# A graph layer on one core: keys by VectorE's own division, constants and first moments in waits for edges, 24 rows compacted aside behind pass 4

## The chip, the core and the metric

The kernel runs on one core of a Trainium2 chip. A core has engines that run side by side, each through its own list of instructions in order: TensorE (PE in the profile, its weight loads PEld), VectorE (DVE), ScalarE (ACT), GpSimd (POOL) and SyncE (SP). SyncE only issues DMA transfers here. GpSimd issues those whose addresses come from a table (indirect gathers) and those that add to what is there. An engine waits for another by semaphores.

The metric is the time of one execution on the device in microseconds (us). Smaller is better.

## What is computed

`N` is 6250 nodes with 128 channels, `E` 206250 edges sorted by `dst`. Cut to what matters:

```python
def _L0_gnn_ref(x, W, b, edge_index):
    src, dst = (edge_index[0], edge_index[1])
    x_i = x[dst]
    x_j = x[src]
    feat = jnp.concatenate([x_i, x_j - x_i], axis=-1)
    msg = feat @ W.T + b
    out = jax.ops.segment_max(msg, dst, num_segments=x.shape[0])
    return jnp.where(jnp.isfinite(out), out, 0.0)
h = jnp.maximum(_layernorm(x, axis=-1), 0.0)
x = x + _L0_gnn_ref(h, L0_gnn_W, L0_gnn_b, edge_index)
```

The message of an edge is A(dst) + B(src), with A = h (W1 - W2)^T + b and B = h W2^T. So the largest message of a node is its A plus the channelwise maximum of B over its sources.

## The kernel before

Partition p owns 49 consecutive destination nodes. Their edges lie together, since edges are sorted by destination, and partition p loads a window of 1792 edges that covers them. Most edges are handled without any gather: sources are numbered as l times 50 plus q (l up to 125, q up to 50), and for each q TensorE builds, by one-hot matrices, the row of B that each destination wants from that q, and VectorE takes maxima. That works for one edge for each destination and q. The edges left over (a second edge of the same destination and q) are rows that GpSimd gathers from B in DRAM, up to 420 for each partition, and VectorE chains them.

The program order is written out by hand: each engine gets its instructions in the order in which the code issues them. The parts are these.

**Edges.** A coarse look at `dst` gives each partition's window start `begin_i` (lines 271 to 278). GpSimd gathers the windows `swin` (src) and `dwin` (dst), lines 284 and 285. SyncE writes one word of each back (line 340), which holds the later loads of x behind the windows.

**Keys.** For each edge, VectorE and ScalarE make l, q and the destination's place `dlc` among the 49, and from them the key `KA` = 64 dlc + q2 (lines 483 to 498). ScalarE computes `big`, the quotient that VectorE rounds to `vm` (line 490). `T` in the trace is the store `T3`, whose parts (`eq`) hold the integer temporaries, and later the comparison results.

**Comparisons.** 41 lags: VectorE compares `KA` with itself shifted by the lag (line 535), TensorE adds the results up in PSUM `dup` by a matmul with the identity (line 524). At hand-chosen lags (`among`, from line 560) other work is laid between: the moments for the next 10 columns of x (`moments`: bn_stats, bn_aggr), the root and reciprocal (`scales`, `inverse`), and, by `ln(n)`, the next `n` steps of the layer norm and the product.

**Layer norm and product.** `micro` is a list of 75 steps, three to a cycle: `turn` (transposes of two columns), `product` (a bias matmul and two with `wT`, giving B in the first 128 columns and A in the last), `remainder`. Six of the steps run before the comparisons, 40 in them, the others behind. Every ten columns SyncE writes B to `Bt` and A to `XA`, and GpSimd adds x to `XA` (`add_x`).

**Compaction.** ScalarE counts the left-over edges (line 594). A scan gives each the distance it has to move, and eleven passes (`pass_`, lines 632 and 633) move them by 1, 2, 4 and so on. Ahead of pass 6 (`EP` = 6, `early`) the first `EW` = 48 rows (`GB` = 6 groups of `U` = 8) are taken aside out of blocks of 128 and put together in a tree of copies. Their list goes to `ridx` (line 655), and GpSimd issues their gathers while the passes go on. The full list follows at line 717. `turned` transposes the keys on TensorE through a PSUM pool of two tiles (`ps_t`).

**Checks.** Counts in `badc` tell whether the inputs fit the fast path (`finite`, `found`, `apart`, lines 731 to 765).

**Main loop.** 325 pairs (13 tiles of nodes, 25 pairs of q). For each pair: one-hots by TensorE and ScalarE (lines 905, 906), products (line 983), maximum on VectorE (989). `more_rows(to)` lays between them `stream_step`, VectorE's chain over gathered rows (line 157), up to row `to`, and further gathers. Gathered rows live in a ring of `GB` groups in `X`: the next group is issued when the oldest group has been chained, and SyncE copies a chained group to `M` (line 164). `pieces` makes the one-hot inputs OHQ and OHD on VectorE (lines 800 to 807). At last 49 gathers bring the results `R` out of `M` (`get_rows`), VectorE joins them with the main loop's maxima and x (lines 1021, 1022), and SyncE and ScalarE store them.

Of the kernel before, what the change touches and what calls it, by code (L numbers as in the profile page):

```python
# [8 lines left out]
F32 = mybir.dt.float32  # L9
# [10 lines left out]
P = 128  # L20
# [18 lines left out]
U = 8  # L39
# [14 lines left out]
def gnn_kernel(tc, x, src, dst, W, b, out):  # L54
# [17 lines left out]
    EP = 6  # L72
    EW = GB * U
    SETS = (WIN - EW - (1 << EP)) // (2 << EP) + 1
    assert EW + (1 << EP) <= 2 << EP and SETS <= 16 and WIN % (2 << EP) == 0
# [17 lines left out]
    with ExitStack() as ctx:  # L93
# [13 lines left out]
        with ExitStack() as body:  # L107
# [58 lines left out]
            with ExitStack() as pre:  # L166
# [77 lines left out]
                kbias = pool.tile([P, 1], F32, name="kbias")  # L244
                bsel = pool.tile([P, L], F32R, name="bsel")
                brow = pool.tile([P, 2 * C], F32R, name="brow")
                V.memset(kbias, (1 - Q) * 0.5 / Q)
# [37 lines left out]
                gather(dwin, dst.rearrange("(e o) -> e o", o=1), begin_i[:, 0:1])  # L285

# [35 lines left out]
                moments(0, GQ)  # L322
                scales(0, GQ)()
                V.tensor_copy(identb, ident)
                neg = pool.tile([P, P], BF16, name="neg")
                V.tensor_scalar_mul(neg, identb, -100.0)
                negb = pool.tile([P, P], BF16, name="negb")
                V.tensor_scalar_mul(negb, identb, -1.0)
# [3 lines left out]
                V.tensor_copy(IQ, row[:, 0, :Q].rearrange("p (q o) -> p q o", o=1).to_broadcast([P, Q, NBLK]))  # L332
                V.tensor_copy(IL, row[:, 1, :LD].rearrange("p (q o) -> p q o", o=1).to_broadcast([P, LD, NBLK]))
                for i in range(NBLK):
                    V.tensor_scalar_add(IW[:, :, i], row[:, 1, :WN], float(near[i]))
                V.tensor_scalar(nbias, row[:, 0], -2.0, -1.0, op0=ALU.mult, op1=ALU.add)
# [94 lines left out]
                def product(k):  # L431
                    pm = steps[k]["pm"] = ps_m.tile([P, 2, 2 * C], F32, name="pm")
                    T_.matmul(pm[:L], bsel, brow.rearrange("k (o c) -> k o c", o=1).to_broadcast([P, 2, 2 * C]),
                              start=True, stop=False)
                    for j in range(2):
                        T_.matmul(pm[:L, j], hT[k % 2][:, j, :L], wT, start=False, stop=j == 1)  # L436
                    if k + 1 < NP_:
                        scaled(k + 1)
                    g, o = where(k)
                    A_.copy(Bp[:L, 0, 2 * k:2 * k + 2], pm[:L, :, :C])  # L440
                    A_.copy(stage[:, g, o:o + 2], pm[:L, :, :C])
# [31 lines left out]
                scaled(0)  # L473
                ln(2)

# [7 lines left out]
                A_.activation(big, sq, AF.Identity, scale=1.0 / Q, bias=kbias)  # L483
                A_.activation(s16, sq, AF.Identity, bias=nthr)
                V.tensor_scalar(d16, dwin, nthr, None, op0=ALU.add)
                V.tensor_scalar(dlc, d16, 0.0, float(LD + 1), op0=ALU.max, op1=ALU.min)
                dlc64 = eq[0].bitcast(I16)
                lq = eq[1].bitcast(I16)
                V.tensor_scalar(dlc64, dlc, 64.0, None, op0=ALU.mult)
                V.tensor_scalar(vm, big, MAGIC, -(MAGIC + L), op0=ALU.add, op1=ALU.add)  # L490
                V.tensor_scalar(lq, vm, float(-Q), None, op0=ALU.mult)
                V.tensor_tensor(q2, s16, lq, ALU.add)
                V.tensor_tensor(KA[:, 64:], dlc64, q2, ALU.add)
                ln(2)
                A_.activation(big, sq, AF.Copy, scale=float(1 << PB))
                ln(2)
# [68 lines left out]
                among[4] += [sel_rows]  # L565
                later = {}
                for q0, at_ in ((GQ, (1, 2, 3, 5)), (2 * GQ, (8, 10, 11, 13)), (3 * GQ, (17, 19, 20, 22)),
# [5 lines left out]
                for i in range(1, 41):  # L573
                    among[i].append(lambda: ln(1))
# [16 lines left out]
                less = junk[0]  # L591
                for i in range(2):
# [3 lines left out]
                make_sel(30, 40)  # L596

# [39 lines left out]
                def early():  # L637
# [3 lines left out]
                    F, FM = (swin[:, j * 16 * EW:(j + 1) * 16 * EW].rearrange("p (m w) -> p m w", w=EW) for j in range(2))  # L641
# [15 lines left out]
                    for _ in range(GB):  # L657
                        gather_group()
# [22 lines left out]
                for i in range(5):  # L681
                    rest[i].append(lambda i=i: ln(4 if i < 4 else len(micro)))
# [13 lines left out]
                for i in range(11):  # L696
# [3 lines left out]
                    for f in rest[i]:  # L700
# [17 lines left out]
                                op1=ALU.bitwise_and)  # L718
                sdl = u[:, OV:GR + OV]
# [5 lines left out]
                V.tensor_scalar(s, s, -0.5, FMAX, op0=ALU.add, op1=ALU.mult)  # L725
                make_sel(40, Q)
# [4 lines left out]
                spread_begin()  # L731
                finite(w_sb, 2 * C, P, 18)
                finite(bsrc[:1], C, 1, 20)
                found()
                apart()
# [3 lines left out]
                V.tensor_scalar(badc[:, 4:5], over_, 0.0, None, op0=ALU.is_lt)  # L739
                V.tensor_tensor(less[:, 1:], d16[:, 1:], d16[:, :WIN - 1], ALU.is_lt)  # L740
# [11 lines left out]
                for v, op, o in ((VMAX, ALU.is_lt, badc[:L, 16:17]), (-VMAX, ALU.is_gt, badc[:L, 17:18])):  # L752
                    V.tensor_scalar(fin_[:L, :Q], mv[:, :, 1], v, None, op0=op, op1=ALU.add, accum_out=o)
# [346 lines left out]
```

## Time and profile before

| what | us |
|---|---|
| median of three runs (771.83 to 774.6) | 774.47 |
| the profiled execution's own time | 775.43 |
| its span, from the first instruction to the last | 773.6 |
| busy: TensorE / VectorE / ScalarE / GpSimd | 642.1 / 720.9 / 482.9 / 504.0 |
| edges' windows asked for (GpSimd) | 10.99 and 12.41 |
| first comparison (VectorE) | 29.91 |
| first pass | 101.81 |
| first row gather (GpSimd) | 128.79 |
| first maximum of the main loop (VectorE) | 176.82 |
| last row gather, last result gather (GpSimd) | 722.97, 763.78 |

A row of a timeline reads: start and duration in us, engine, line of the code, operation, output and input with their shapes, the count, and in brackets the idle time of the engine just before it with what ended it ("issue" where the profile shows nothing that it waited for). A row that merges several neighbours gives the time of all of them. A row of a group gives the count, the busy time in all, the mean of one in ns, and behind the bar the idle time before them. The engine with the highest busy share need not be the one that sets the end. That is told by who waits for whom, and where.

### The profile page before, as it was taken

How to read it: one execution, taken by the hardware profiler on the slowest of the kernel's cores; microseconds unless marked ns; L12 is line 12 of the kernel's file. 1: busy time of each engine (PE TensorE's matmuls, PEld its weight loads, DVE VectorE, ACT ScalarE, POOL GpSimd, SP SyncE). 2: the span in 40 equal slices, each digit the busy share in tenths (PEclk: the TensorE clock that was granted, in tenths of full speed). 3: DMA queues.
4: the chain of work that ended last, by engine and by line, in shares of the span. 5: the costliest groups of instructions: out<-in, count | busy, mean ns of one | idle time of the engine just before them, and what ended most of it. 6: DMA issues, size and time to landing. Idle time of an engine off the chain costs nothing.

```text
span 773.6 us, 11963 instructions
## 1 busy us (share of the span) xinstructions
PE 642.1 (83%) x3643; PEld 466.6 (60%) x3643; DVE 720.9 (93%) x1304; ACT 482.9 (62%) x1035; POOL 504.0 (65%) x522
## 2 busy tenths in 40 slices
PE   0799884649999898899989898999989898996860
PEld 0455553537667676666767666766767576775750
DVE  6999799987999999999999999999999999997773
ACT  3655683226789999565666657575666667674500
POOL 4000003877777777777777777777777777777764
PEclk9999997759999999999999999999999999998875
DMA  6542444123443433334343243434343233433593
GB/s 196 133 101 67 101 104 108 46 61 94 109 116 103 117 104 92 104 106 116 106 117 101 83 114 104 116 106 115 104 116 101 83 113 103 116 106 106 160 227 123
DMA packets 83699, 85.05 MB, mean 110 GB/s; under 512 B 9996, under 2 KB 71554, under 8 KB 83372
## 3 DMA queue, kind: packets, MB, share of 16 engines
q1 hardware_dynamic: 66951, 47.36, 21.7%
q0 software_dynamic: 16080, 35.93, 17.5%
q10 hardware_dynamic: 596, 0.92, 0.4%
q8 instruction: 30, 0.49, 0.3%
q14 instruction: 42, 0.34, 0.1%
HBM read 46.76 MB, written 40.47 MB: 113 GB/s over the span
## 4 chain that ended last, share of the span: by engine, by line
DVE 25%; PE 16%; issue 15%; ACT 9%; DMA 9%; POOL 3%; DVEq 0%; POOLq 0%
DVE acc L989 15%; PE ps L983 9%; DVE X L157 6%; DMA X<-Bt,ridx 6%; ACT oh L906 5%; PE z L905 4%; ACT counted L996 4%; DMA R<-M,last_e 3%; PE pv L837 2%; POOL X L87 2%; POOL R L87 1%; DVE OHQ L800 1%; DVE acc L987 1%; DVE OHD L807 1%; DVE OHD L804 0%
## 5 line engine op out<-in xcount | busy, mean ns | idle before, releaser
L87 POOL DMA_INDIRECT X<-Bt,ridx x420 | 440.7, 1049 | 131.7 <-issue 45.4
L906 ACT ACTIVATE oh<-z 126x490 fp32r<-126x490 f32 (+1 forms) x650 | 340.1, 586 | 162.6 <-PE z L905 161.3
L983 PE MATMUL ps<-oh,Bp 126*128 126x490 f32 (+1 forms) x1300 | 392.5, 425 | 40.1 <-DVE acc L989 38.9
L989 DVE TENSOR_TENSOR acc<-acc,ps 128x980 f32<-128x980 f32 (+1 forms) x312 | 361.1, 1157 | 8.3 <-PE ps L983 6.8
L983 PEld LDWEIGHTS ps<-oh,Bp 126*128 126x128 f32 x1300 | 239.3, 193 | 135.0 <-DVE acc L989 90.8
L905 PE MATMUL z<-Vb,Sel 128*126 128x490 f16 (+1 forms) x650 | 195.3, 375 | 12.4 <-ACT oh L906 9.7
L157 DVE SCALAR_TENSOR_TENSOR X<-X,slim 128x128 f32<-128x128 f32 x419 | 146.8, 350 | 9.2 <-issue 7.6
L905 PEld LDWEIGHTS <-Sel 128*126 128x126 f16 x650 | 86.8, 142 | 32.1 <-issue 3.9
L837 PEld LDWEIGHTS <-OHQ 128*128 128x128 bf16 x910 | 62.5, 161 | 17.8 <-issue 16.9
L837 PE MATMUL pv<-OHD,OHQ 128*128 128x28 bf16 (+1 forms) x896 | 67.2, 228 | 4.5 <-DVE OHD L807 4.4
L444 POOL DMA_DIRECT2D XA<-in_x x5 | 4.5, 902 | 94.3 <-DMA XA<-acc 94.3
L800 DVE TENSOR_TENSOR OHQ<-T,IQ 128x1092 bf16<-128x1092 bf16 (+5 forms) x104 | 62.2, 605 | 0.0
L87 POOL DMA_INDIRECT R<-M,last_e x49 | 48.3, 985 | 17.0 <-issue 11.3
L996 ACT ACTIVATE counted<-lane_dl,nbias 128x556 bf16<-128x556 int32 x50 | 42.6, 851 | 0.1
L524 PE MATMUL dup<-T,identb 128*128 128x512 bf16 (+1 forms) x168 | 39.8, 363 | 3.0 <-DVE T L535 2.8
L436 PE MATMUL pm<-wT,hT 128*125 128x256 f32 x100 | 27.7, 402 | 2.7 <-ACT hT L425 2.6
L524 PEld LDWEIGHTS <-identb 128*128 128x128 bf16 x168 | 16.2, 99 | 18.8 <-issue 6.4
L633 DVE COPY_PREDICATED pk<-big,pk 128x1927 int32<-128x1927 int32 (+12 forms) x13 | 22.9, 1759 | 0.4
L436 PEld LDWEIGHTS pm<-wT,hT 128*125 128x125 f32 x100 | 19.5, 198 | 6.1 <-ACT hT L425 3.7
L419 ACT ACTIVATE hs<-X,nmr,rstd 125x128 f32<-125x128 f32 x50 | 22.0, 494 | 0.5 <-DVE nmr L306 0.5
L535 DVE TENSOR_TENSOR T<-KA,KB 128x1792 bf16<-128x1792 int16 x21 | 21.5, 1081 | 0.2 <-PE dup L524 0.2
L535 DVE TENSOR_TENSOR T<-KA 128x1792 bf16<-128x1792 int16 x20 | 20.8, 1080 | 0.0
(272 smaller groups left out, 452.1 us busy)
## 6 DMA issues: line engine op xcount, KB each, us to landing
M<-X SPq DMA_DIRECT2D x52, 512.0 KB
X<-Bt,ridx POOLq DMA_INDIRECT x420, 2.5
XA<-in_x POOLq DMA_DIRECT2D x5, 625.0 KB, 6.1
ownb<-Bt SPq DMA_DIRECT2D x12, 245.0 KB
X<-in_x SPq DMA_DIRECT2D x5, 560.0 KB
Bt<-acc SPq DMA_DIRECT2D x4, 560.0 KB
XA<-acc SPq DMA_DIRECT2D x4, 560.0 KB
out_x<-R SPq DMA_DIRECT2D x8, 224.0 KB
```

Source lines behind the costliest of these rows:

```text
L87: G_.indirect_dma_start(out=o, out_offset=None, in_=table, in_offset=bass.IndirectOffsetOnAxis(ap=idx, axis=0))
L157: V.scalar_tensor_tensor(G[:, j], state["prev"], slim[:, k:k + 1], G[:, j], op0=ALU.min, op1=ALU.max)
L436: T_.matmul(pm[:L, j], hT[k % 2][:, j, :L], wT, start=False, stop=j == 1)
L524: T_.matmul(dup[:, c0:c1], w, e[:, c0:c1], start=first, stop=last)
L535: V.tensor_tensor(e, KA[:, 64:], i1, ALU.is_equal)
L800: V.tensor_tensor(OHQ[:, :nl, a:z], over(TQ, z - a), iq, ALU.is_equal)
L837: T_.matmul(o, w, m, start=False, stop=True, skip_group_check=True)
L905: T_.matmul(z[:L + 1, :n], Sel[:, i + j], Vb[t % 2][:, :n], start=True, stop=True)
L906: A_.activation(oh[:, :n], z[:L + 1, :n], AF.Relu)
L983: T_.matmul(ps[:, j, :n], Bp[:, e, i + j], oh[j][:, :n], start=e == 0, stop=e == 1)
L989: V.tensor_tensor(a, a, ps[:, :, :n], ALU.max)
L996: A_.activation(counted.bitcast(BF16)[:, :NS], lane_dl, AF.Sign, scale=2.0, bias=nbias[:, c:c + 1], accum_out=ends[:, c:c + 1])
```

## The change

It changes eight things.

1. The quotient is no longer ScalarE's: VectorE divides `swin` and writes int16, which rounds (`l16`); `lq`, `q2` and `vm` come from it. `KA` is built in place. ScalarE's first pass in this part is now `s16`. The pass that writes `big` for the packed word moves to lag 7.
2. The constants (identb, neg, negb, IQ, IL, IW, nbias) go from behind the first moments to right behind the edges' gathers.
3. The first ten moments are split: five before the keys, five among them, and the scales behind.
4. No layer-norm step runs before the comparisons; inside, each of the 41 lags has one step and every fifth two (49 instead of 40).
5. `EP` 5, `EW` 24: the first 24 rows are taken aside behind pass 4, out of blocks of 64. The other three groups of the ring are issued behind the full list.
6. The checks of W, of the variances and the matmul of `spread_begin` move to the wait for the count; the check of the heads moves ahead, the others change their order.
7. The bias matmul covers only the columns of A.
8. `more_rows` takes 4 rows instead of 10 before the first pair, and then reaches 16 by the fourth pair.

```diff
-    EP = 6
-    EW = GB * U
+    EP = 5
+    EW = 3 * U
...
                 gather(dwin, dst.rearrange("(e o) -> e o", o=1), begin_i[:, 0:1])
+                V.tensor_copy(identb, ident)
...
+                V.tensor_copy(IQ, row[:, 0, :Q].rearrange("p (q o) -> p q o", o=1).to_broadcast([P, Q, NBLK]))
...
-                moments(0, GQ)
-                scales(0, GQ)()
-                V.tensor_copy(identb, ident)
...
+                moments(0, GQ // 2)
...
-                    T_.matmul(pm[:L], bsel, brow.rearrange("k (o c) -> k o c", o=1).to_broadcast([P, 2, 2 * C]),
-                              start=True, stop=False)
+                    T_.matmul(pm[:L, :, C:], bsel, brow[:, C:].rearrange("k (o c) -> k o c", o=1).to_broadcast([P, 2, C]),
+                              start=True, stop=False, skip_group_check=True)
...
-                scaled(0)
-                ln(2)
...
-                A_.activation(big, sq, AF.Identity, scale=1.0 / Q, bias=kbias)
+                lq = eq[1].bitcast(I16)
+                l16 = eq[0].bitcast(I16)
                 A_.activation(s16, sq, AF.Identity, bias=nthr)
+                V.tensor_scalar(l16, sq, 1.0 / Q, (1 - Q) * 0.5 / Q, op0=ALU.mult, op1=ALU.add)
+                V.tensor_scalar(lq, l16, float(-Q), float(Q * L), op0=ALU.mult, op1=ALU.add)
+                V.tensor_tensor(q2, s16, lq, ALU.add)
+                V.tensor_scalar(vm, l16, float(-L), None, op0=ALU.add)
+                moments(GQ // 2, GQ)
+                scaling = scales(0, GQ)
                 V.tensor_scalar(d16, dwin, nthr, None, op0=ALU.add)
                 V.tensor_scalar(dlc, d16, 0.0, float(LD + 1), op0=ALU.max, op1=ALU.min)
-                V.tensor_scalar(dlc64, dlc, 64.0, None, op0=ALU.mult)
-                V.tensor_scalar(vm, big, MAGIC, -(MAGIC + L), op0=ALU.add, op1=ALU.add)
-                V.tensor_scalar(lq, vm, float(-Q), None, op0=ALU.mult)
-                V.tensor_tensor(q2, s16, lq, ALU.add)
-                V.tensor_tensor(KA[:, 64:], dlc64, q2, ALU.add)
-                ln(2)
-                A_.activation(big, sq, AF.Copy, scale=float(1 << PB))
-                ln(2)
+                scaling()
+                scaled(0)
+                V.tensor_scalar(KA[:, 64:], dlc, 64.0, None, op0=ALU.mult)
+                V.tensor_tensor(KA[:, 64:], KA[:, 64:], q2, ALU.add)
...
+                among[7] += [lambda: A_.activation(big, sq, AF.Copy, scale=float(1 << PB))]
...
-                for i in range(1, 41):
-                    among[i].append(lambda: ln(1))
+                for i in range(SH):
+                    among[i].append(lambda i=i: ln(2 if i % 5 == 4 else 1))
...
+                spread_begin()
...
                 make_sel(30, 40)
+                finite(w_sb, 2 * C, P, 18)
...
-                    for _ in range(GB):
+                    for _ in range(EW // U):
                         gather_group()
...
+                for _ in range(GB - EW // U):
+                    gather_group()
...
-                more_rows(10)
+                more_rows(4)
...
-                    more_rows(GR * (k + 1 - wait) // (len(pairs) - wait - early))
+                    more_rows(max(GR * (k + 1 - wait) // (len(pairs) - wait - early), min(3 * k + 7, 16)))
```

The order of VectorE between the first moments and the first comparisons, before (`d_343` is d16, `s_344` s16, `q_342` q16):

```order
L294 BN_STATS stats<-X 125x6 x10
...
L324 CAST identb<-ident 128x128
...
L485 TENSOR_SCALAR d_343<-pk,nthr 128x1792
L486 TENSOR_SCALAR dlc__175<-d_343 128x1792
L489 TENSOR_SCALAR T_82<-dlc__175 128x1792
L490 TENSOR_SCALAR vm<-big 128x1792
L491 TENSOR_SCALAR T_82<-vm 128x1792
L492 TENSOR_TENSOR T_82<-s_344,T_82 128x1792
L493 TENSOR_TENSOR KA<-T_82 128x1792
```

and of the change (its own line numbers; `d_314` is d16, `s_315` s16):

```order
L302 BN_STATS stats<-X 125x6 x5
L304 BN_AGGR mv<-stats 125x2 x5
L480 TENSOR_SCALAR T_82<-swin 128x1792
L481 TENSOR_SCALAR T_82<-T_82 128x1792
L482 TENSOR_TENSOR T_82<-s_315,T_82 128x1792
L483 TENSOR_SCALAR vm<-T_82 128x1792
L302 BN_STATS stats<-X 125x6 x5
L304 BN_AGGR mv<-stats 125x2 x5
L486 TENSOR_SCALAR d_314<-pk,nthr 128x1792
L487 TENSOR_SCALAR dlc__175<-d_314 128x1792
```

The work on src now stands ahead of the work on dst, and the constants have left this stretch.

VectorE where the rows are taken aside, before:

```order
L632 TENSOR_SCALAR big<-pk 128x1896
L633 COPY_PREDICATED pk<-big,pk 128x1896
L509 MEMSET tick 128x1
L642 MEMSET mend_i 128x1
L644 TENSOR_SCALAR swin<-pk 128x672
...
L655 TENSOR_SCALAR ridx<-swin 128x48
L659 SCALAR_TENSOR_TENSOR s_344<-dup,vm 128x1792
L632 TENSOR_SCALAR big<-pk 128x1864
```

and of the change:

```order
L643 MEMSET mend_i 128x1
L645 TENSOR_SCALAR swin<-pk 128x672
...
L656 TENSOR_SCALAR ridx<-swin 128x24
L660 SCALAR_TENSOR_TENSOR s_315<-dup,vm 128x1792
L633 TENSOR_SCALAR big<-pk 128x1896
L634 COPY_PREDICATED pk<-big,pk 128x1896
L504 MEMSET tick 128x1
L633 TENSOR_SCALAR big<-pk 128x1864
```

The pass of width 1896 (pass 5) has moved from ahead of `ridx` to behind it.

GpSimd's list from the last adds of x on, before:

```order
L444 DMA XA<-in_x 125x1280 x4
L87 DMA mend<-M,mend_i 128x128
L87 DMA X<-Bt,ridx 128x128 x48
L444 DMA XA<-in_x 125x1280
L87 DMA X<-Bt,ridx 128x128 x80
```

and of the change:

```order
L441 DMA XA<-in_x 125x1280 x4
L87 DMA mend<-M,mend_i 128x128
L87 DMA X<-Bt,ridx 128x128 x24
L441 DMA XA<-in_x 125x1280
L87 DMA X<-Bt,ridx 128x128 x104
```

The last add of x stands behind 24 row gathers instead of 48; the gathers are the same in number.

65 lines of the change are left out of this document (29 added, 36 removed).

## The prediction

> **What bounds the kernel now.** I read the page first, then GpSimd's own timeline (each row: start, duration, engine, line, operation, output and input, count, and in brackets the idle time just before it with what ended it), then the timelines of VectorE, TensorE and SyncE at the places that GpSimd's told me of.
>
> ```profile
> span 773.6 us, 11963 instructions
> ...
> L87 POOL DMA_INDIRECT X<-Bt,ridx x420 | 440.7, 1049 | 131.7 <-issue 45.4
> ...
> L800 DVE TENSOR_TENSOR OHQ<-T,IQ 128x1092 bf16<-128x1092 bf16 (+5 forms) x104 | 62.2, 605 | 0.0
> ...
> L87 POOL DMA_INDIRECT R<-M,last_e x49 | 48.3, 985 | 17.0 <-issue 11.3
> ```
>
> The page gives VectorE 93% and GpSimd only 65%, yet GpSimd sets the end. It issues 420 row gathers and 49 result gathers. Each takes 0.94 us at its best and has about 0.30 us of idle time ahead of it, so 1.25 us is the least from one to the next. Its timeline from first to last:
>
> ```profile
> 128.79 0.99 POOL L87 DMA_INDIRECT X<-Bt,ridx  x1 [4.07 <-ACT KB L678]
> ...
> 161.81 1.48 POOL L87 DMA_INDIRECT X<-Bt,ridx  x1 [0.30 <-issue]
> ...
> 210.80 0.99 POOL L87 DMA_INDIRECT X<-Bt,ridx  x1 [0.30 <-DVE OHQ L800]
> ...
> 722.97 0.94 POOL L87 DMA_INDIRECT X<-Bt,ridx  x1 [0.30 <-issue]
> ...
> 763.78 0.94 POOL L87 DMA_INDIRECT R<-M,last_e  x1 [0.30 <-issue]
> ```
>
> From 128.79 to 764.72 us the gap is 0.30 again and again: of the 470 rows between them only three, near 740, show more than 0.4 us. GpSimd waits for nobody, so the end is its first gather plus 636 us plus 8.9 us for the last landing, maximum and store. VectorE, full from 172 to 700 us, has to wait for gathers near the end:
>
> ```profile
> 710.02 0.35 DVE L157 SCALAR_TENSOR_TENSOR X<-X,slim 128x128 f32<-128x128 f32 x1 [4.02 <-issue]
> ...
> 722.89 0.40 DVE L157 SCALAR_TENSOR_TENSOR X<-X,slim 128x128 f32<-128x128 f32 x1 [3.55 <-issue]
> ```
>
> So the change is worth what it moves GpSimd's first row gather forward, less what it slows the gathers behind it. VectorE's work in the main loop counts only where it would fall behind.
>
> **Keys and constants.** VectorE before the first lag comparison (L535):
>
> ```profile
> 10.54 0.15 DVE L278 CAST begin_i<-begin 128x1 int32<-128x1 f32 x1
> ...
> 13.97 0.29 DVE L309 TENSOR_TENSOR w<-w_sb 128x128 f32<-128x128 f32 x1 [3.28 <-DMA w_sb<-in_L_gnn_W]
> ...
> 15.39 2.03 DVE L294 BATCH_NORM_STATS2 stats<-X 125x6 f32<-125x128 f32 x10
> ...
> 18.80 0.22 DVE L324 CAST identb<-ident 128x128 bf16<-128x128 f32 x1
> ...
> 21.63 1.15 DVE L485 TENSOR_SCALAR d<-pk,nthr 128x1792 int16<-128x1792 int32 x1
> 22.82 0.63 DVE L486 TENSOR_SCALAR dlc__175<-d 128x1792 bf16<-128x1792 int16 x1
> ...
> 25.26 1.09 DVE L490 TENSOR_SCALAR vm<-big 128x1792 bf16<-128x1792 f32 x1 [1.15 <-ACT big L483]
> 26.39 0.63 DVE L491 TENSOR_SCALAR T<-vm 128x1792 int16<-128x1792 bf16 x1
> 27.12 1.09 DVE L492 TENSOR_TENSOR T<-s,T 128x1792 int16<-128x1792 int16 x1
> 28.25 1.09 DVE L493 TENSOR_TENSOR KA<-T 128x1792 int16<-128x1792 int16 x1
> ...
> 29.32 0.68 DVE L498 TENSOR_SCALAR q<-T,nthr 128x1792 bf16<-128x1792 int16 x1
> 29.91 2.09 DVE L535 TENSOR_TENSOR T<-KA 128x1792 bf16<-128x1792 int16 x2
> ```
>
> The constants take 18.80 to 21.63, 2.83 us, and move into the 3.28 us wait for w_sb, which they fit. If w_sb came at once they would cost their 2.83 again. From 15.39, start to start: five moments 1.35 (half of the ten, which last to 18.09), ready at 16.74. The edges' src must have landed:
>
> ```profile
> 16.80 0.25 SPq L340 DMA_DIRECT2D SC<-swin  x1
> ...
> 25.11 1.79 ACT L484 ACTIVATE s<-swin,nthr 128x1792 int16<-128x1792 int32 x1
> ```
>
> SyncE's marker write starts at 16.80, so src lands just before; the division starts at 16.85. It reads int32 and writes int16 as L485 does: 1.19. Then the product like L491, 0.70, and the sum like L492, 1.13; its other input is ScalarE's 1.79 us pass, now first in line at 16.85 and ready beside it. After that vm 0.66, five moments 1.35, d16 1.19, dlc 0.66, the two small scale instructions 0.31, dlc times 64 0.66, the sum into KA 1.07, the rest 0.59. The total is 9.51, so the first comparison starts at 26.36 instead of 29.91: 3.55 us earlier. The root that the scales need has d16 and dlc to hide in.
>
> An unknown: GpSimd generates the two edge gathers at 10.99 and 12.41, now under these constants. Their price lies between nothing and what such a gather loses under VectorE's compaction passes:
>
> ```profile
> L87 POOL DMA_INDIRECT X<-Bt,ridx x4 | 9.5, 2381 | 1.2 <-issue 0.9 <-ACT T L666 0.3
> ```
>
> These four (129.86 to 139.75 us, passes 6 to 8) take 2.38 us instead of 0.94, 1.44 more each: 2.9 us for two at worst. The constants are short and mostly of small shape, so I take 0.3. The Trainium skill (page "SBUF — State Buffer", section "SBUF: two separate sides") says that GpSimd cannot write a DMA's descriptors while VectorE holds the shared port in a two-port mode. These rows agree in kind; this is the rule that speaks against the change.
>
> **The 41 comparisons.** Here TensorE ends last. ScalarE's count (L594) follows its last matmul, and VectorE waits for ScalarE:
>
> ```profile
> 80.33 0.92 PE L524 MATMUL dup<-T,identb 128*128 128x512 bf16 x4
> ...
> 82.87 0.48 PE L433 MATMUL pm<-brow,bsel 128*125 128x512 f32 x1
> 83.18 1.02 PE L436 MATMUL pm<-wT,hT 128*125 128x256 f32 x4
> ...
> 84.05 0.92 PE L524 MATMUL dup<-T,identb 128*128 128x512 bf16 x4
> ...
> 89.62 1.69 PE L524 MATMUL dup<-T,identb 128*128 128x512 bf16 x8
> ...
> 91.40 1.01 ACT L594 ACTIVATE T<-dup,pos_h 128x896 bf16<-128x896 f32 x1 [0.93 <-issue]
> ...
> 93.52 0.35 DVE L598 TENSOR_SCALAR flow<-level,listed 128x128 f32<-128x128 f32 x1 [2.32 <-ACT T L594]
> ```
>
> Three comparisons with one layer-norm cycle of three steps take TensorE 3.72 us (80.33 to 84.05), against 3 x 1.02 on VectorE. Of the 3.72 about 0.69 each belong to the comparisons and 1.65 to the cycle. The bias on half the columns cuts 82.87 to 83.18 by about half, to a cycle of 1.50. But the six steps that ran before the comparisons now run inside: 49 there instead of 40. In the last 13 comparisons, with no moments on VectorE to let TensorE catch up, 13 x 0.69 + 5.2 x 1.50 = 16.8 replaces 13 x 1.24 = 16.1, 0.7 more, and it enters them further behind. I take 1.1 lost. The bounds are nothing and 2.5 (nine more steps are 3 cycles, 4.5, less 0.15 saved in each of 13 old ones).
>
> The checks of W and of the variances move into the 2.32 us wait before L598. Without that wait they would cost about 1.7.
>
> **The rows aside.** Pass 5 of VectorE (its L632 here, its L633 behind it) and the compaction aside:
>
> ```profile
> 119.80 1.15 DVE L632 TENSOR_SCALAR big<-pk 128x1896 int32<-128x1896 int32 x1
> ...
> 123.28 0.51 DVE L644 TENSOR_SCALAR swin<-pk 128x672 int32<-128x672 int32 x1
> ...
> 125.20 0.36 DVE L652 TENSOR_SCALAR swin<-swin 128x336 int32<-128x336 int32 x1
> ...
> 127.36 0.19 DVE L652 TENSOR_SCALAR swin<-swin 128x48 int32<-128x48 int32 x1
> ...
> 127.83 0.19 DVE L655 TENSOR_SCALAR ridx<-swin 128x48 int32<-128x48 int32 x1
> ```
>
> It begins where pass 5 began, 119.80 instead of 123.28: 3.48 us earlier. Its widths are 672, 336, 168, 72, 48, 24 instead of 672, 336, 144, 96, 48. That is one more level like the one from 127.36 to 127.83, and little else, so 0.4 longer. GpSimd's first row gather then comes at 128.79 - 3.55 + 0.3 + 1.1 - 3.48 + 0.4 = 123.56, 5.23 us earlier.
>
> But it now also runs under pass 5, 3.4 us (119.80 to 123.28 without the two small memsets). At 2.38 + 0.30 per gather that pass gives 1.27 gathers, worth 1.27 x 1.25 = 1.59 in free time: 1.8 lost. The net is **3.4 us**. The bounds of this loss are 0 and 3.4 (no gather at all in pass 5).
>
> The 24 rows last GpSimd past 150 us, and the full list (L717, at 147 before, some 2 us earlier now) is ready by then. The add of x, now issued behind 24 gathers instead of 48, costs GpSimd the same instruction. The layer norm must have written Bt before a gather reads it: it ends earlier by the front's shift and by one cycle (nine steps more done inside the comparisons, six fewer done before them), so it stays ahead.
>
> **VectorE and the ring.** VectorE reaches the main loop earlier by 3.55 - 0.3 - 1.1 - 0.4 = 1.75, by the 1.7 of the moved checks, and by a wait that the earlier heads check fills:
>
> ```profile
> 160.03 0.16 DVE L766 CAST mend_i<-pm 127x1 int32<-127x1 f32 x1 [1.18 <-PE pm L763]
> ```
>
> That is 4.6, more than the 3.4 of GpSimd, so the 7.6 us that VectorE waits at 710 and 722 grow and it stays off the end. In the other direction GpSimd needs a free place in the ring of 48 rows:
>
> ```profile
> 202.44 0.39 SPq L164 DMA_DIRECT2D M<-X  x1
> ```
>
> The second group's copy left at 202.44, and the gather that reuses its place came at 210.80: 8.4 us in hand, more with 16 rows now done by the fourth pair. Hidden so far, the row steps cost nothing here; if GpSimd came to wait there, each microsecond would be lost at the end.
>
> **Sum.** The span goes from 773.6 to 770.2, the profiled execution from 775.43 to 772.0. That execution lies 1.0 above the median of the runs, 774.47, so the predicted median is 774.5 - 3.4 = **771.1 us**, 0.44% less.
>
> **Rivals.**
> - *The collisions cost less.* Gathers run at full pace in pass 5 (5.2 gained, 769.3), or the passes block them only during L632: 5.23 - 1.15 = 4.1, 770.4. Against it: the four gathers above lost 5.8 us under three L632 of 3.2 us together. The skill's rule on the two-port modes, named above, gives the second case if only L632 is in such a mode; these rows do not bear that out.
> - *The edge gathers are locked out by the constants.* 2.9 instead of 0.3: 0.8 gained, 773.7. For it: GpSimd's slow gathers; against it: the constants' tiny sizes.
> - *The early gathers don't start early,* held by Bt or ScalarE. Then only the 1.75 of the front remains, 772.7. For it: the trace names ScalarE as what ended GpSimd's wait at 128.79, 0.6 us after ridx was written.
> - *Slower: the gathers of the main loop fall differently on VectorE's OHQ instructions.* The 420 gathers lost 420 x (1.049 - 0.940) = 46 us to slowed issues. The gather at 161.81 took 1.48 where VectorE makes OHQ (104 times, 0.6 us each). With GpSimd bound, every such hit moves the end. Seven per cent more hits take the whole 3.4 back; a sixth more, 7.8 us, gives 778.9. For it: the change shifts VectorE by 4.6 and GpSimd by 3.4 against each other, and the first 16 rows are spread otherwise. Against it: the instructions are the same in number, and over a hundred of them chance evens out.
>
> **How the numbers follow.** I give the forecast 0.45 (its own range 769.0 to 773.0), cheaper collisions 0.25, the edge gathers 0.13, the late start 0.05, slower 0.12. A measurement of this kernel can tell about 0.5%, 3.9 us, from no change: under 770.6 counts as faster, over 778.3 as slower. The forecast lies so close to that edge that I give four tenths of it to faster: 0.18 + 0.24 = 0.42 faster. The rest of the forecast, the edge gathers and the late start make 0.46 within, and 0.12 are slower. The range for eight in ten: down to 767.0 (the 5.2 of unslowed gathers and some 2 of fewer hits), up to 776.0 (TensorE at its bound takes 1.4 more, the edge gathers at theirs 2.6 more, which ends at 775.1, and 1 of more hits).
>
> **What would show it.** The first L535 at about 26.4 to 26.7; ScalarE's count at 89 (1.1 of the 3.2 lost); the mend gather at 117 and the first row gather at 123.6; gathers of 2 to 3 us in pass 5; gaps of 0.30 on GpSimd to the end; its last gather 3.4 us earlier than 763.78; VectorE's waits near the end longer than 7.6. I am wrong if GpSimd shows gaps over 0.4 in the main loop, if the mean of its row gathers moves away from 1.05, or if the first one is not between 122 and 126.

## The result, and the profile after

| | before | changed |
|---|---|---|
| median of 10 runs each, us | 773.97 (771.83 to 774.6) | 769.62 (766.3 to 772.96) |
| profiled execution, us | 775.43 | 769.23 |
| its span, us | 773.6 | 767.5 |

The ratio is 0.995, with a 95% interval of 0.9931 to 0.9969: 4.35 us or 0.56% by the medians, where 3.4 us was forecast. The two spans differ by 6.1 us, more than the medians do, since the profiled execution of before (775.43) was slower than all ten of its runs in the table. The changed kernel run again beside other experiments (h0_control below) gave 769.52 against 774.08, ratio 0.9928 (0.9909 to 0.9947). Six of the runs below (f0 to g1) fell on two chips on which every kernel, the one before included, takes some 1,085 us; their ends are not compared with the others.

The page of the changed kernel, its first line and the groups that answer to those shown of before:

```profile
span 767.5 us, 11957 instructions
...
L87 POOL DMA_INDIRECT X<-Bt,ridx x420 | 440.6, 1049 | 132.1 <-issue 40.2
...
L87 POOL DMA_INDIRECT R<-M,last_e x49 | 49.6, 1012 | 16.4 <-issue 11.6
...
L798 DVE TENSOR_TENSOR OHQ<-T,IQ 128x1092 bf16<-128x1092 bf16 (+5 forms) x104 | 61.4, 598 | 0.0
```

The row gathers cost what they did, 440.6 us against 440.7. GpSimd didn't become faster; it started earlier. Its timeline (start, duration, engine, line, operation, output and input, count, idle time before it with what ended it):

```profile
117.33 1.18 POOL L87 DMA_INDIRECT mend<-M,mend_i  x1 [7.73 <-DMA Bt<-acc]
122.96 0.99 POOL L87 DMA_INDIRECT X<-Bt,ridx  x1 [4.45 <-DVE ridx L656]
124.25 1.74 POOL L87 DMA_INDIRECT X<-Bt,ridx  x1 [0.30 <-issue]
126.29 2.45 POOL L87 DMA_INDIRECT X<-Bt,ridx  x1 [0.30 <-issue]
129.06 3.08 POOL L87 DMA_INDIRECT X<-Bt,ridx  x1 [0.32 <-issue]
132.44 2.96 POOL L87 DMA_INDIRECT X<-Bt,ridx  x1 [0.30 <-ACT T L667]
135.71 2.43 POOL L87 DMA_INDIRECT X<-Bt,ridx  x1 [0.30 <-issue]
138.44 1.00 POOL L87 DMA_INDIRECT X<-Bt,ridx  x1 [0.30 <-ACT T L667]
...
162.91 0.94 POOL L87 DMA_INDIRECT X<-Bt,ridx  x1 [0.30 <-DMA X<-Bt,ridx]
163.85 1.02 POOL L441 DMA_DIRECT2D XA<-in_x  x1
165.17 1.24 POOL L87 DMA_INDIRECT X<-Bt,ridx  x1 [0.30 <-issue]
...
718.65 0.94 POOL L87 DMA_INDIRECT X<-Bt,ridx  x1 [0.30 <-issue]
...
758.55 0.94 POOL L87 DMA_INDIRECT R<-M,last_e  x1 [0.30 <-issue]
```

The first row gather starts 5.83 us earlier (122.96 against 128.79), and VectorE's ridx releases it. The last row gather is 4.32 earlier (718.65 against 722.97), the last result gather 5.23 (758.55 against 763.78). Between the first gather and the last the idle times are 0.30 us, but for three of 0.5 to 0.9 us near 740, where before had three as well. In h0_control the first and last are at 122.86 and 760.66: the start repeats, the end scatters by 2 us. Five gathers now take 1.7 to 3.1 us, where before had four.

The first 24 row gathers as a group in before, and then in the changed kernel (count; busy us, mean ns of one; idle before them):

```profile
L87 POOL DMA_INDIRECT X<-Bt,ridx x24 | 31.9, 1329 | 11.1 <-issue 5.2 <-ACT KB L678 4.1 <-DMA X<-Bt,ridx 1.5
```
```profile
L87 POOL DMA_INDIRECT X<-Bt,ridx x24 | 33.9, 1412 | 11.5 <-DVE ridx L656 4.4 <-issue 4.0 <-DMA X<-Bt,ridx 1.8
```

These lose 2.0 us more. So 5.83 - 2.0 = 3.8 us is left of the shift at the 25th gather (168.00 before; 165.17 now, with the add of x, 1.02 us, already done, which before comes later).

VectorE and GpSimd at the front of the changed kernel:

```profile
12.32 1.81 DVE L292 TENSOR_SCALAR IW<-row 128x14 bf16<-128x14 f32 x14
13.42 0.73 DVE L293 TENSOR_SCALAR nbias<-row 128x50 f32<-128x50 f32 x1
13.71 0.45 DVE L317 TENSOR_TENSOR w<-w_sb 128x128 f32<-128x128 f32 x1
...
16.52 1.06 DVE L480 TENSOR_SCALAR T<-swin 128x1792 int16<-128x1792 int32 x1
...
25.56 2.08 DVE L530 TENSOR_TENSOR T<-KA 128x1792 bf16<-128x1792 int16 x2
```
```profile
10.97 1.12 POOL L87 DMA_INDIRECT swin<-in_src,begin_i  x1 [6.20 <-DVE identb L284]
12.39 0.94 POOL L87 DMA_INDIRECT pk<-in_dst,begin_i  x1 [0.31 <-issue]
13.34 0.62 POOL L91 IOTA kk<- 128x556 f32 x1
```

The constants fill the wait for w_sb, which is gone: L317 starts at 13.71 (13.97 before). The two edge gathers keep their 1.12 and 0.94 us. The first comparison starts at 25.56, 4.35 us earlier than before's 29.91. At the end of the comparisons, on TensorE, ScalarE and VectorE:

```profile
86.86 1.69 PE L519 MATMUL dup<-T,identb 128*128 128x512 bf16 x8
```
```profile
88.63 1.01 ACT L591 ACTIVATE T<-dup,pos_h 128x896 bf16<-128x896 f32 x1 [0.93 <-issue]
```
```profile
90.75 0.34 DVE L599 TENSOR_SCALAR flow<-level,listed 128x128 f32<-128x128 f32 x1 [1.53 <-ACT T L591]
```

ScalarE's count is 2.77 us earlier (91.40 before), so 1.58 of the front's 4.35 were lost in the comparisons. VectorE still waits 1.53 us behind the checks that moved in.

### The profile page after: what moved, and what is told of

Read it like the earlier page. It is cut to its first block, busy times and chain, and to the rows that moved or that the text cites. A ratio compares the mean times of both kernels' runs of the same rounds, so it can differ in the third digit from the quotient of the medians.

```text
span 767.5 us, 11957 instructions
## 1 busy us (share of the span) xinstructions
PE 634.3 (83%) x3636; PEld 462.9 (60%) x3643; DVE 721.8 (94%) x1306; ACT 481.6 (63%) x1034; POOL 505.3 (66%) x522
## 4 chain that ended last, share of the span: by engine, by line
DVE 29%; PE 21%; issue 15%; DMA 5%; ACT 4%; POOL 2%; DVEq 0%; POOLq 0%
DVE acc L987 18%; PE ps L981 12%; DVE X L157 7%; PE z L903 5%; PE pv L835 4%; DMA X<-Bt,ridx 3%; ACT oh L904 2%; DMA R<-M,last_e 2%; ACT counted L994 2%; DVE OHQ L798 2%; POOL R L87 1%; POOL X L87 1%; DVE OHD L802 1%; DVE R L1019 1%; DVE acc L985 1%
## 5 line engine op out<-in xcount | busy, mean ns | idle before, releaser
L87 POOL DMA_INDIRECT X<-Bt,ridx x420 | 440.6, 1049 | 132.1 <-issue 40.2
L157 DVE SCALAR_TENSOR_TENSOR X<-X,slim 128x128 f32<-128x128 f32 x419 | 143.5, 342 | 7.6 <-DMA X<-Bt,ridx 3.6
L835 PEld LDWEIGHTS <-OHQ 128*128 128x128 bf16 x910 | 62.6, 162 | 16.3 <-issue 15.4
L87 POOL DMA_INDIRECT R<-M,last_e x49 | 49.6, 1012 | 16.4 <-issue 11.6
L421 PE MATMUL pt<-ident,hs 125*128 125x125 f32 x50 | 12.6, 303 | 10.0 <-ACT hs L416 9.0
```

What stands on the lines that cost most here:

```text
L87: G_.indirect_dma_start(out=o, out_offset=None, in_=table, in_offset=bass.IndirectOffsetOnAxis(ap=idx, axis=0))
L157: V.scalar_tensor_tensor(G[:, j], state["prev"], slim[:, k:k + 1], G[:, j], op0=ALU.min, op1=ALU.max)
L835: T_.matmul(o, w, m, start=False, stop=True, skip_group_check=True)
```

## The experiments

All kernels are the changed kernel with one edit. Of the six runs on the chips that take 1,085 us only the rows ahead of about 165 us are read, as GpSimd doesn't set the end there.

**e1_rows48: the early compaction undone.**

```
-    EP = 5
-    EW = 3 * U
+    EP = 6
+    EW = GB * U
```

> The changed kernel with the early compaction put back: 48 rows aside behind pass 5 instead of 24 behind pass 4, all else as changed. Theory (GpSimd's first row gather sets the end, less what the passes slow): the first row gather comes about 3.1 us later than in the changed kernel (126.1 instead of 123.0), its first 24 gathers lose 2.0 us less, so the end comes 1.1 us later: 770.7 us. Rival (the early rows are given back completely in the passes): 769.6, no difference. Rival (the collisions of pass 5 would have come anyway): 3.1 later, 772.7.

771.38 us (771.04 to 771.99), ratio to before 0.9972 (0.9959 to 0.9984). The first row gather starts at 125.93. The first 24 as a group, and the 49th, which here stands behind the add:

```profile
L87 POOL DMA_INDIRECT X<-Bt,ridx x24 | 31.7, 1320 | 11.1 <-ACT T L667 5.0 <-issue 4.9 <-DMA X<-Bt,ridx 0.9
```
```profile
196.99 1.04 POOL L87 DMA_INDIRECT X<-Bt,ridx  x1 [0.30 <-issue]
```

The start is 3.0 us later and the collisions 2.2 to 2.3 less. The 49th gather starts 0.9 us later than the changed kernel's 196.09 (0.5 later than h0_control's 196.46). By the rows the early compaction is worth 0.5 to 0.9 us of its 3.0; by the ratios 1.7 to 3.4, with intervals of 1 us and more on either side. The rows speak against the 3.1 us of the last rival; the times alone would leave it standing.

**e2_pool_late: GpSimd held between the 24th and the 25th gather.**

```
+                for _ in range(28):
+                    G_.memset(X[:, 6272:6400], 0.0)
                 for _ in range(GB - EW // U):
                     gather_group()
```

> The changed kernel with 28 small memsets on GpSimd (about 0.18 us each, 5 us in all) between the 24th row gather and the 25th; VectorE's work is the same. Theory (GpSimd sets the end, nothing waits in between): the whole 5 us at the end, 774.6. Rival (VectorE's main loop sets the end and GpSimd has room): 769.6 to 771.

776.43 us, ratio 1.0034 (1.002 to 1.0048). The memsets took 0.275 us each, not 0.18:

```profile
165.16 7.71 POOL L721 MEMSET X<- 128x128 f32 x28
173.36 1.04 POOL L87 DMA_INDIRECT X<-Bt,ridx  x1 [0.50 <-issue]
```

From the 24th gather's start to the 25th's it is 9.74 us instead of 2.26, so 7.5 us were added. The ratio is 0.0084 to 0.0106 above the changed kernel's two, 6.5 to 8.2 us. The last result gather starts at 765.96, 7.4 later than the changed kernel's and 5.3 later than h0_control's. So the delay of GpSimd arrives at the end, all of it as far as a scatter of 2 us lets one tell.

**e3_vector_late: VectorE held ahead of its main loop.**

```
+                for _ in range(2):
+                    V.tensor_tensor(big, sq, sq, ALU.add)
                 V.tensor_scalar(badc[:, 2:3], nres, ...)
```

> The changed kernel with two added passes on VectorE (int32 x int32 into f32, 128 x 1792, about 2.2 us each, 4.4 in all) ahead of the checks behind the passes; GpSimd's instructions are the same. Theory (GpSimd sets the end): VectorE's main loop starts 4.4 us later and its waits near the end, 6.8 us, shrink by that; the time stays, 769.6 to 770.3. Rival (the gain came from VectorE reaching the main loop 5.1 us earlier): 774.0.

771.49 us, ratio 0.9966 (0.9954 to 0.9979): 1.2 to 2.9 us above the changed kernel's two ratios. Against the first of them the intervals overlap, against h0_control's they don't. The theory had said no change and the rival 4.4; the measured value lies between. The passes took 2.02 us each, and VectorE's main loop began at 159.22 instead of 155.20. GpSimd has two waits that the changed kernel doesn't have, for places in its ring, and its first 24 gathers take 35.5 us instead of 33.9 to 34.0:

```profile
328.02 1.09 POOL L87 DMA_INDIRECT X<-Bt,ridx  x1 [0.65 <-DVE OHQ L800]
...
339.13 0.94 POOL L87 DMA_INDIRECT X<-Bt,ridx  x1 [1.17 <-DVE X L157]
```

That is 0.35 + 0.87 beyond the usual 0.30, and 1.5 to 1.6 from the gathers that ran under the added passes: 2.7 together, and the last result gather (761.36) is 2.8 later than the changed kernel's, but only 0.7 later than h0_control's. By these rows VectorE's lateness costs time through GpSimd's gathers and its ring, and not one for one; the size is not settled. VectorE's own waits near the end remain, 3.8 us.

**e4_ln_even and f1_ln45: fewer layer-norm steps among the comparisons** (41 and 45 instead of 49).

```
-    among[i].append(lambda i=i: ln(2 if i % 5 == 4 else 1))
+    among[i].append(lambda i=i: ln(1))
...
-                ln(2)
+                ln(4)
...
-                ln(6)
+                ln(8)
```

That is e4; f1 has this alone:

```
-    among[i].append(lambda i=i: ln(2 if i % 5 == 4 else 1))
+    among[i].append(lambda i=i: ln(2 if i % 10 == 6 else 1))
```

> The changed kernel with one layer-norm step in each comparison (41 instead of 49 inside), four more steps behind them beside the scan, the rest in the passes. Theory (TensorE ends last in the comparisons and lost 1.6 us there to the nine steps more): ScalarE's count at 87.1 to 87.6 instead of 88.6, everything behind it 1.0 to 1.5 us earlier, 768.3. Rival (VectorE's own comparisons set that stage, TensorE's steps are covered): 769.6. Rival (the layer norm's last rows then land too late for the first row gather): 770 or more, and GpSimd waits for Bt.

> The changed kernel with 45 layer-norm steps among the comparisons instead of 49 (the extra step at each tenth comparison, not each fifth), the other four behind. In the run with 41, eight steps fewer brought ScalarE's count 1.2 us forward against the first comparison but Bt's last rows landed too late for the first gather (124.78 instead of 122.6). Theory (two limits: TensorE 0.15 us per step in the comparisons, ScalarE's chain of 0.81 us per step behind them, with 4.4 us in hand before the first gather): count 0.6 us earlier, Bt still 1 us ahead of the gather, end 0.6 us earlier than the control. Rival (the steps behind the comparisons are already on the path, with no slack): 3.2 - 0.6 = 2.6 us later than the control, the gather released by Bt.

e4: 771.27 us, ratio 0.9969 (0.9957 to 0.9981). From the first comparison (26.03) to the count (87.90) it is 61.87 us, 1.2 less than the changed kernel's 63.07. But ten profiles with 49 steps (below) scatter from 62.4 to 63.3, so the eight steps are worth 0.6 to 1.4 us, 0.8 at their median. TensorE's term is real, and not sharply known. The last rival decided. The layer norm's last copy of Bt, on SyncE, and the first row gather:

```profile
119.59 0.80 SPq L455 DMA_DIRECT2D Bt<-acc  x2
```
```profile
124.78 0.99 POOL L87 DMA_INDIRECT X<-Bt,ridx  x1 [6.67 <-DMA Bt<-acc]
```

ridx was written at 121.65; without the wait the gather would have followed at 122.6. f1, on one of the other chips, was late as well: count 62.22 us after the first comparison (62.44 in its control), Bt's last copy at 119.49, ridx at 122.33, first gather at 125.56 instead of some 123.3. Here the profile names a pass of VectorE that ended just before as what released the gather; that it was Bt is an inference. The edit meant to leave Bt 1 us ahead, and the gather came some 2 late.

One thing in f1 isn't the edit's. TensorE's granted clock was 0.50 from 91 to 101 us there, in e4 only from 90.5 to 94. It falls in unaltered kernels too: over 96 to 110 us it was 0.51 in h0_control and 1.00 in the profile of the result. The same four matmuls of the layer norm, first in the changed kernel and then in h0_control:

```profile
99.45 1.06 PE L433 MATMUL pm<-wT,hT 128*125 128x256 f32 x4
```
```profile
100.55 1.91 PE L433 MATMUL pm<-wT,hT 128*125 128x256 f32 x4
```

Bt's last copy is issued 24.7 us behind the count where the clock stays at 1.00 (113.36 in the changed kernel; the same 24.7 in e2 and h1), and 28.3 us behind it in h0_control (116.76). A step of the layer norm behind the comparisons costs 0.81 us at full clock (a cycle of three 2.43, 99.45 to 101.88). So e4's eight steps make 24.7 + 6.5 = 31.2 of its 31.7 us: e4 is late by its steps. f1's four make 27.9 of its 30.9: about 3 us, by this estimate, go with the clock, more than the 2 by which the gather was late. Eight steps can't be moved out of the comparisons without holding the gathers; whether four can, at full clock, f1 doesn't show.

**f2_rows16: 16 rows aside behind pass 3.**

```
-    EP = 5
-    EW = 3 * U
+    EP = 4
+    EW = 2 * U
```

> The changed kernel with 16 rows aside behind pass 3 instead of 24 behind pass 4. The compaction aside begins at about 113.5 us instead of 117.1 and lasts some 0.9 longer (896 wide, one level more): first row gather at 120.3, 2.7 us earlier than in the control; pass 4 costs its gathers 2.0 (as pass 5 did). Theory (a pass gives back what its gathers lose, the rest stays): end 0.7 us earlier than the control. Rival (nothing is left of an earlier start in the passes): same as the control. Rival (Bt's last rows hold the first gather): 1.5 to 2 us later than the theory says, GpSimd released by Bt.

Compared by rows with f0_control. The compaction aside took 6.2 us instead of 5.0, ridx came at 120.41 instead of 121.92 although this run's count was 0.88 late, and the first gather started at 121.36 (122.87), 2.4 us earlier counted from there. The gathers under the passes, of which the last three take a whole pass each:

```profile
122.65 1.74 POOL L87 DMA_INDIRECT X<-Bt,ridx  x1 [0.30 <-issue]
124.70 2.52 POOL L87 DMA_INDIRECT X<-Bt,ridx  x1 [0.30 <-issue]
127.52 3.15 POOL L87 DMA_INDIRECT X<-Bt,ridx  x1 [0.30 <-issue]
130.98 3.10 POOL L87 DMA_INDIRECT X<-Bt,ridx  x1 [0.30 <-issue]
134.38 2.98 POOL L87 DMA_INDIRECT X<-Bt,ridx  x1 [0.30 <-ACT T L667]
```

The twelfth gather starts at 145.45 (144.67 in the control) and the 25th at 163.86 (163.41), so with the 0.88 taken off 0.1 and 0.4 us are left. A further pass is hardly worth its compaction.

**f3_bias_all: the bias over all columns again.**

```
-    T_.matmul(pm[:L, :, C:], bsel, brow[:, C:]...to_broadcast([P, 2, C]), ...)
+    T_.matmul(pm[:L], bsel, brow...to_broadcast([P, 2, 2 * C]), ...)
```

> The changed kernel with the bias product over all 512 columns again, 0.31 us instead of 0.20 in each layer-norm cycle, nothing else. Theory (TensorE ends last in the second half of the comparisons, some eight cycles there without a wait): ScalarE's count 0.9 us later, and the end with it. Rival (VectorE's comparisons set that stage): no difference. Upper bound: all 16 cycles, 1.8 us.

From the first comparison (25.72) to the count (89.23) it is 63.51 us. The ten profiled runs with the half bias and 49 steps have 62.4 to 63.3, median 62.6. That is 0.9 above the median, as the theory had it, but only 0.2 above the highest of ten: one run doesn't show the size, and hardly that there is a gain. In this run the profile names Bt as what released the first gather (123.78, some 0.2 us later than ridx would have let it start), with no step of the layer norm moved; TensorE's clock over 96 to 110 us was 0.76.

**f0_control and g0_control, g1_add_early: the other chips, and the add of x moved ahead of the first row gather.**

```
                     gather(mend, M[:P, :], mend_i[:, 0:1])
+                    add_x(Q - GQ)
...
-                add_x(Q - GQ)
```

> The changed kernel itself, unaltered, beside the next three runs and the kernel before on the same chip: ratio to the kernel before 0.994 to 0.996 (769.6 us at 774.0). First row gather at 123.0 us, waits of VectorE for gathers near the end about 7 us. Both theories expect this; it gives the yardstick for the others.

> The changed kernel itself, unaltered, as the yardstick of this call: ratio to the kernel before 0.995 (769.6 us at 774.0), within 0.993 to 0.997. First row gather at 122.9 us, GpSimd's gaps 0.30 to the end.

> The changed kernel with GpSimd's last add of x (1.0 us and the gap ahead of it, 1.32 in all, now between the 24th row gather and the 25th) issued ahead of the first row gather, where GpSimd waits 4.45 us for VectorE's compaction aside; nothing else. Theory (GpSimd's chain from the first row gather on sets the end): the row gathers from the 25th on 1.3 us earlier, end 1.3 us earlier than the control, 768.3. Rival (VectorE's main loop sets the end too): no difference. Rival (the last rows of XA land late and the add holds up the first row gather): the first row gather later than 122.9, end later by that less 1.3.

On these chips the kernel before took 1,087.81 and 1,084.32 us and the changed one 1,078.87 and 1,088.51 (ratios 0.9817, from 0.9751 to 0.9883, and 1.0041, from 0.9965 to 1.0116). Two ratios of one change that exclude each other tell nothing of the ends. The front is as elsewhere (first row gather at 122.87 and 122.38). In g1 the add ran at 121.38, and the 25th gather started 39.33 us after the first, against 40.51 in g0: the 1.2 us are saved there. How these chips differ, in f0_control on TensorE, VectorE and GpSimd:

```profile
172.86 0.91 PE L666 MATMUL ptb<-identb,s 128*128 128x32 bf16 x14 [26.86 <-issue]
...
177.17 0.37 PE L499 MATMUL dup<-zero,identb 128*128 128x256 bf16 x1 [1.67 <-issue]
179.98 0.37 PE L499 MATMUL dup<-zero,identb 128*128 128x256 bf16 x1 [2.44 <-issue]
```
```profile
198.50 0.16 DVE L764 CAST mend_i<-pm 127x1 int32<-127x1 f32 x1 [35.83 <-PE pm L736]
```
```profile
225.43 1.00 POOL L87 DMA_INDIRECT X<-Bt,ridx  x1 [32.23 <-DVE OHD L805]
```

**h0_control and h1_add_early: the same pair on a chip like the first.**

> The changed kernel unaltered once more, as the yardstick of this call: 0.995 of the kernel before (within 0.993 to 0.997), first row gather at 122.9 us, if the chip runs the kernel before in 774 us; on a chip that takes 1085 us for it, as in the last two calls, GpSimd doesn't set the end and only the rows before 160 us can be compared.

> The changed kernel with GpSimd's last add of x ahead of the first row gather, as in g1_add_early. There the 25th row gather came 1.33 us after the 24th's end of issue less, and the first one was not held up. Theory (GpSimd's chain sets the end): 1.3 us earlier than the control, ratio to the kernel before 0.9933. Rival (VectorE's main loop sets the end too): the control's ratio. Rival (it holds only where GpSimd sets the end): on a chip that takes 1085 us, no difference in the end.

h0: 769.52 us, ratio 0.9928 (0.9909 to 0.9947). h1: 770.3 us, ratio 0.9943 (0.9921 to 0.9964). In h1:

```profile
119.31 0.89 POOL L441 DMA_DIRECT2D XA<-in_x  x1 [0.28 <-issue]
123.48 1.06 POOL L87 DMA_INDIRECT X<-Bt,ridx  x1 [3.28 <-DVE ridx L657]
...
164.72 0.96 POOL L87 DMA_INDIRECT X<-Bt,ridx  x1 [0.31 <-issue]
```

The 25th gather follows the first by 41.24 us, in h0 by 42.32 (122.86 to 165.18). So 1.1 us are saved in the order, but the time isn't measurably shorter: the medians go the other way by 0.8 us, the intervals overlap, and the first gather itself moves by 0.6 us between these two. The theory's 1.3 us at the end is not borne out. No version was shown to beat the changed kernel.

## Why the prediction held, step by step

- **GpSimd sets the end.** Held. e2 shows it from GpSimd's side (7.5 us added, 6.5 to 8.2 at the end), e3 from VectorE's (4.0 later, 1.2 to 2.9 at the end, by way of GpSimd's own gathers and ring). The end scatters by 2 us from run to run, so that h1's 1.1 us could not be seen there.
- **The front, 3.55 less 0.3 for the edge gathers: 26.7 forecast, 25.56 measured.** Too little by 1.1 in this profile. The other twelve profiles with this front start the first comparison at 25.57 to 26.37; the median of all thirteen is 26.04. Two sizes were off. From the division to the first comparison it is 9.04 us, not 9.51, and the lock-out of the edge gathers, for which 0.3 was taken and 2.9 was the worst, didn't occur: both kept their 1.12 and 0.94 us. In this profile the division also began early, at 16.52; in most of the others it began at 16.7 to 17.3. No run undid the front alone; what it is worth is read from the rows.
- **TensorE in the comparisons, 1.1 lost of 0 to 2.5.** 1.58 in this profile. The ten profiles with 49 steps and the half bias take 62.4 to 63.3 us from the first comparison to the count; before took 61.49. That is 0.95 to 1.84 lost, and 1.15 at their median. e4 (0.6 to 1.4 back for eight steps fewer) shows that the steps inside take part in it.
- **The compaction aside: begins 3.48 earlier, 0.4 longer.** From the first instruction aside to ridx 4.94 us instead of 4.55: the 0.4. The first gather was forecast at 123.56 and came at 122.96, the front's surplus less TensorE's. In the changed kernel VectorE's ridx released it, so ScalarE and Bt didn't. The prediction's "so it stays ahead" put no price on TensorE's clock. e4's gather started 5.2 us behind the issue of Bt's last copy; by that the margin is some 4 us in this profile, 0.9 in h0_control and nothing in g0_control (copy at 117.17, gather at 122.38), where the clock over 96 to 110 us was 0.50.
- **Pass 5: 1.8 lost of 0 to 3.4.** 2.0. The rows now say how it comes about. VectorE's passes beside the gathers above:

```profile
124.03 1.14 DVE L633 TENSOR_SCALAR big<-pk 128x1896 int32<-128x1896 int32 x1
125.20 2.26 DVE L634 COPY_PREDICATED pk<-big,pk 128x1896 int32<-128x1896 int32 x1
...
127.49 1.13 DVE L633 TENSOR_SCALAR big<-pk 128x1864 int32<-128x1864 int32 x1
128.66 2.23 DVE L634 COPY_PREDICATED pk<-big,pk 128x1864 int32<-128x1864 int32 x1
...
130.92 1.10 DVE L633 TENSOR_SCALAR big<-pk 128x1800 int32<-128x1800 int32 x1
132.05 2.17 DVE L634 COPY_PREDICATED pk<-big,pk 128x1800 int32<-128x1800 int32 x1
```

  The gathers that begin at 126.29 and 129.06, under a COPY_PREDICATED, end at 128.74 and 132.14, 0.12 us after the TENSOR_SCALAR behind it (128.62, 132.02); in f2 the gathers of 124.70, 127.52, 130.98 and 134.38 do the same. The gather of 124.25, begun under a TENSOR_SCALAR, ends at 125.99, 0.82 us behind it and under a COPY_PREDICATED. So in these rows a COPY_PREDICATED holds a gather that begins under it, and not one that is under way. A pass of 3.4 us yields one gather, worth 1.25, not the 1.27 gathers taken. This refutes the rival that only L632 of before blocks (1.15 lost). The Trainium skill (page "SBUF — State Buffer", section "Who interferes with whom") has VectorE's two-input instructions contend with GpSimd's reads, and tensor_scalar, in its two-port modes, with GpSimd's instructions of any kind; these ends agree with both together, though the page doesn't name COPY_PREDICATED.
- **The main loop's collisions, the rival on the slower side.** It did not happen; the difference came out on the other side. The 396 row gathers behind the first 24 took 408.8 us before and 406.7 in the changed kernel (407.7 in h0), where that rival needed 3.4 us more to take the gain back.
- **VectorE and the ring.** VectorE reached the main loop 5.1 us earlier (155.20 against 160.30; 4.6 forecast). Its waits for gathers near the end should have grown beyond 7.6 us; they came to 6.8 in the changed kernel and 8.2 in h0. That step is not borne out. No gather of the changed kernel waited for the ring, and e3 shows that with 4.0 us less two would have: VectorE's earlier start is cover for the ring, not a gain by itself. How much of it the moved checks must give was not tried. The new spread of the first row steps was not tried alone.

The sum by the rows of the profiled pair: 4.35 (front) - 1.58 (comparisons) + 3.45 (one pass) - 0.4 (aside) = 5.8 at the first gather, and 3.8 behind pass 5. To the last result gather, with all 469 issued in both, the later row gathers add 2.1, the result gathers take 1.3 (49.6 against 48.3 us) and their idle time gives back 0.6: 5.2, and 5.23 was measured. Another 0.9 came behind the last result gather (8.0 us to the end of the span instead of 8.9; h0_control has 8.8), which makes the spans' 6.1.

So the forecast's 3.4 for GpSimd's start held to 0.4 us: behind pass 5 it was 3.8, since the front gave 1.1 more than forecast, of which the comparisons took back 0.5 and pass 5 took 0.2. The further 1.4 to the last result gather has no term in the sum. It came in the main part from collisions that fell otherwise in the main loop, the prediction's own rival with the sign turned round: that was luck. The medians' 4.35 lies between the 3.8 and the 5.2. The measured median, 769.62, lies nearer to the rival with gathers at full pace (769.3) than to the forecast's 771.1, but the rows refute that rival: the gathers in the pass lost 2.0.

## What to carry to other kernels

Look for an in-order engine that is far from busy and yet never waits: its first instruction plus its count times the issue interval is the end, and an edit elsewhere counts by how far it moves that first instruction, here within a scatter of 2 us. Starting such an engine earlier inside a stage that blocks it earns little, here one issue of 1.25 us per pass of 3.4 us, less the dearer preparation. Before an input is pulled forward, look up when the second-latest one lands, in more than one profile: here the layer norm's rows landed some 4 us ahead in one and with no margin in another, and moving eight steps out of the comparisons cost the gathers 2.2 us.

## What the runs showed of the hardware

- VectorE paid, and the edge gathers did not, where the constants met them: the 14 small adds into IW took 1.81 us instead of 1.18, and nbias 0.73 instead of 0.19, beginning under GpSimd's iota at 13.34 and ending 0.19 us after that one's end. The same 1.81 and 0.73 stand in e2 and h0; g0 has 2.20 and 1.13. GpSimd's next iota paid a little too (0.48 us instead of 0.26). The Trainium skill (page "SBUF — State Buffer", section "SBUF: two separate sides") says that of the two whichever starts first holds the shared pair for its whole instruction; the trace agrees, in the direction that the prediction had not weighed.
- TensorE's granted clock behind the comparisons is not the same in every execution of one program: 1.00 from 96 to 110 us in the profile of the result, 0.50 to 0.51 in g0 and h0, where four matmuls of 256 columns took 1.91 us instead of 1.03 to 1.06. Through the layer norm this moved Bt's last copy by up to 3.8 us (113.36 to 117.17). What makes it fall in one execution and not in another is not shown.
- The same program took 1,085 us on two of the four chips of the experiments. The granted clock over the whole span was 0.79 to 0.83 there and 0.93 to 0.95 elsewhere. The first 145 us take the same time; later TensorE and ScalarE stand still up to 27 us, and TensorE starts single matmuls of 0.37 us some 2 to 3 us apart, waiting for nothing that the profile shows. The cause stays open.
- 28 memsets of 128 x 128 on GpSimd back to back, most of them beside VectorE's OHQ and OHD passes, took 0.275 us each; single ones in the kernel's front took 0.19 to 0.28.
